# A gate branch whose product and residual sum become separate steps, with its next head begun one stage earlier and its divisions moved behind the sums

## The chip, the core and the metric

The kernel is one program for one core of a Trainium2 chip, all in fp32. The metric is the device time of one execution in microseconds, the median over the runs shown. One execution was also recorded by the hardware profiler, and all readings of single instructions come from that one.

The core has five instruction streams that each run strictly in their own order: PE (TensorE, matmuls; its weight loads are listed as PEld), DVE (VectorE), ACT (ScalarE), POOL (GpSimd) and SP (SyncE, which here only issues DMAs). An instruction that waits for another engine holds up everything behind it in its own stream.

## The reference

Two stages, each the sum of the residual and a product of two branches, over 4096 tokens (two sequences of 2048) of width 256:

```python
xn = layernorm(x)
s  = local_and_latent_attention(xn)          # first branch
g  = silu(expert_mlp(xn))                    # eight experts, one per token, layernorm at its end
x  = x + s * g
xn = layernorm(x)
s  = attention_and_mlp(xn)                   # second main branch
g  = silu(two_layers(xn))                    # second gate branch
return x + s * g

def two_layers(x):                           # DEPTH = 2, 8 heads of 64
    for l in range(2):
        h = shift_token(x)                   # second half of the channels comes from the token before
        q, k, v = split(h @ wqkv[l])
        q, k = rotary(l2norm(q) * qs, l2norm(k) * ks)
        x = x + local_attention(q, k, v) @ wo[l]          # windows of 128, looking one window back
        h = layernorm(shift_token(x)) * lg + lb
        a, b = split(h @ w1[l] + b1[l])
        x = x + (a * gelu(b)) @ w2[l] + b2[l]
    return x
```

## The kernel before

Tokens lie on the 128 partitions; a tile is 128 tokens, a group is four tiles (`GT = 4`), and there are eight groups (`NG = 8`). The whole program is three stages that follow each other.

1. The first stage, to about 966 us in the profile: for every group the attention branch (`attention(g)`), which stores its rows to the DRAM tensor `rows_s`, and between its steps the sorted tiles of the experts (`experts()`), 39 of them, which store to the DRAM tensor `ysort`.
2. The gate branch, about 966 to 2340 us: sixteen rounds (`NR = 2 * NG`), eight for layer 0 and eight for layer 1. Round r treats the four tiles of one group. Side by side in it stand `attention(r)`, the preparation (`prepare`) of the next tiles' queries and keys, the head of the next round (`gate_head(r + 1)`), and the feed-forward part of the round before (`forward(r - 1)`).
3. The main branch, to the end.

Nothing in this program is left to a scheduler on PE, DVE, ACT and POOL: each engine gets its instructions in the order in which Python emits them (the DMA issues on SP are placed by the framework). Emission order is decided by one helper, `in_turn`. It takes lanes, each a triple `(a, b, steps)`; every step has a weight, the steps of a lane are laid out over the stretch from a to b in proportion to their weights, and all steps of all lanes are then emitted in the order of these places. A step `(3, lambda: None)` emits nothing and only pushes the later ones back. In the first stage places are counted within one group (0 to 1), in the gate branch a unit is one round.

The head of a round of layer 0, `gate_head(r)` with r < 8, is where the first stage's two branches meet and the gate branch gets its input. For its four tiles it

- fetches the input rows `x` and the attention rows `sg` from `rows_s` (SP, 512 KB each),
- gathers the experts' rows `yg` from `ysort` (POOL, four indirect DMAs),
- takes Silu of `yg` in one ACT instruction over all four tiles (L370, with a table load before it),
- per tile multiplies `sg` by `yg` on POOL (L363), adds that to `x` on DVE (L364) and takes the moments (L79 and L80): these are one step, `residual(t)`,
- stores the sum to `rows_r`, forms the reciprocal deviations on POOL (`ln_rsqrt`, L84 and L85) and normalizes on DVE (L88),
- shifts half of the channels by one token with four DMAs to `xs_a` (`shift`), and transposes both halves on PE into `hT` (L384).

The tiles `sg` and `yg` have a single buffer each. For rounds of layer 1 the head is only the shift and the transposes.

In `attention(r)` a block i is half a tile. Its steps are: transposes of the softmax weights (`turn_weights(i)`, L151, copied out as `pt` by ACT and DVE in turn, L69 and L71); then `small(i)`, which is the scores of the next block (L453, softened by DVE at L107, then exponentials on ACT, L473) and the weighted sums of this one (`sum_block(i)`, L483) into two PSUM banks `acc`, of which there are exactly the two that one tile needs. The divisions of a finished tile n (`divide(n)`, DVE: L628, L629, L632) read these banks and are emitted after `turn_weights` of the next tile's first block. So the sums of a new tile may not start before the divisions of the tile before it have read the banks. `turn_out(n)` (L642) and `project_tile(n)` (L658, L667) follow.

In `prepare(m)` the engines alternate on one tile: PE projects (L530, L546), POOL makes the rotated cross terms (`cross`, L563) and a power for the lengths (`lengths`: DVE L572 and L573, then POOL L574), and DVE does the long elementwise steps (`straight` L579, `join` L587, `scale` L590). `forward` is L742, L754, L755 and L764, with L761 and L771 for its sums.

Where the lanes lay before: the head of round 0 is spread over the last group of the first stage (fetch at 0.02, gathers at 0.10, the rest from 0.30 to 0.65); every later head r + 1 lies in round r from its start to 0.45 of it. The experts take a share of each group, 0.35 of the first, all of the next six and 0.1 of the last.

Of the kernel before, what the change touches and what calls it, by code (L numbers as in the profile page):

```python
# [9 lines left out]
ALU = mybir.AluOpType  # L10
# [6 lines left out]
GT = 4  # L17
GW = GT * P
NG = NT // GT
# [11 lines left out]
def kernel(ctx: ExitStack, tc: tile.TileContext, io: dict, col: dict):  # L31
    nc = tc.nc
# [3 lines left out]
    def sb(pool, shape, tag, bufs=None):  # L36
        kw = {} if bufs is None else {"bufs": bufs}
        return pool.tile(list(shape), F32, name=tag, tag=tag, **kw)
# [4 lines left out]
    def bank(tag):  # L43
        return ps.tile([P, 512], F32, name=tag, tag="acc" if tag == "acc" else "b", bufs=2 if tag == "acc" else 6)
# [272 lines left out]
    def group(r):  # L317
        return slice((r % NG) * GT, (r % NG) * GT + GT)
# [20 lines left out]
    def gate_head(r):  # L339

        x = G[:, group(r), :]
        lane = []
        if r < NG:
            d = {}

            def fetch():

                d["mv"] = sb(ph, [P, GT, 2], "h_mv", 2)
                d["rs"] = sb(ph, [P, GT], "h_rs", 2)
                nc.sync.dma_start(x, xin[:, group(r), :])  # L350
                d["sg"] = sb(ph, [P, GT, D], "sg", 1)
                nc.sync.dma_start(d["sg"], rows_s[:, group(r), :])
                d["yg"] = sb(ph, [P, GT, D], "yg", 1)

            def gather(t):
                n = r * GT + t
                nc.gpsimd.indirect_dma_start(
                    d["yg"][:, t, :], None, ysort, bass.IndirectOffsetOnAxis(ap=ati[:, n : n + 1], axis=0)
                )

            def residual(t):

                nc.gpsimd.tensor_tensor(d["sg"][:, t, :], d["sg"][:, t, :], d["yg"][:, t, :], ALU.mult)  # L363
                nc.vector.tensor_tensor(x[:, t, :], x[:, t, :], d["sg"][:, t, :], ALU.add)  # L364
                ln_moments(ph, d["mv"], t, [x[:, t, :]])

            lane.append((0.1, fetch))
            lane += [(0.3, lambda t=t: gather(t)) for t in range(GT)]
            lane.append((3, lambda: None))
            lane.append((1, lambda: nc.scalar.activation(d["yg"], d["yg"], AF.Silu)))  # L370
            lane += [(1, lambda t=t: residual(t)) for t in range(GT)]
            lane.append((0.1, lambda: nc.sync.dma_start(rows_r[:, group(r), :], x)))
            lane.append((1, lambda: ln_rsqrt(d["rs"], d["mv"], 1e-5)))
            lane.append((2, lambda: None))
            for t in range(GT):
                lane.append((1, lambda t=t: normalize(x[:, t, :], x[:, t, :], d["mv"], d["rs"], t)))
        lane.append((0.1, lambda: shift(ph, "xs_a", r, x)))

        def turn(c):
            if r not in heads:  # L380
                heads[r] = sb(ph, [P, 2, GW], "hT", 2)
            tp = bank("tp")
            for t in range(GT):
                nc.tensor.transpose(  # L384
                    tp[:, t * P : (t + 1) * P], shifted["xs_a", r][:, t, :] if c else x[:, t, 0:P], ident
                )
            copy(c, heads[r][:, c, :], tp)

        return lane + [(1, lambda: turn(0)), (2, lambda: None), (1, lambda: turn(1))]
# [16 lines left out]

    pools = {}

    def gate_branch():
        NR, NM = 2 * NG, 2 * NT  # L410
        wo, w1, w2 = {}, {}, {}

# [199 lines left out]
        def turn_weights(i):  # L612
            turns[i] = turned(pools["tasks"], scores.pop(i))

        def sum_block(i):
            n, blk = i // 2, i % 2
            if not blk:
                accs[n] = [
                    bank("acc")[:, 0 : 4 * (DH + 1)].rearrange("p (b u d) -> p b u d", b=2, u=2) for _ in range(2)
                ]  # L620
            keys = [(m, b) for m in (n - 1, n) for b in range(2)][blk : blk + 3][3 - min(3, i % (2 * TPB) + 1) :]
            collect64(turns.pop(i), accs[n], blk, [tiles[m]["v"][:, b, :, :] for m, b in keys])

        def divide(n):
            acc = accs.pop(n)
            rz = sb(pools["tasks"], [P, 2, 2, 2], "rz")
            for w in range(2):
                nc.vector.tensor_copy(rz[:, w, :, :], acc[w][:, :, :, DH])  # L628
            nc.vector.reciprocal(rz, rz)  # L629
            o = outs[n] = sb(pools["tasks"], [P, 2, 2, 2, DH], "o")  # L630
            for w in range(2):
                nc.vector.tensor_tensor(  # L632
                    o[:, :, :, w, :], acc[w][:, :, :, 0:DH], bc(rz[:, w, :, :], 3, [P, 2, 2, DH]), ALU.mult
                )
# [41 lines left out]
        def attention(r):  # L676
            lane = []
            for i in range(2 * GT * r, 2 * GT * (r + 1)):

                n, odd = i // 2 - 1, i % 2  # L680

                def turn(i=i, n=n, odd=odd):
                    turn_weights(i)
                    if n >= 0 and not odd:
                        divide(n)

                def small(i=i):

                    if i + 1 < 2 * NM:
                        score(i + 1)  # L690
                    sum_block(i)

                lane += [(1, turn), (1, lambda: None), (1.5, small)]
                if odd:
                    lane.append((1, lambda n=n: project_tile(n) if n >= 0 else None))
                else:
                    lane += [(0.5, lambda: None), (0.5, lambda n=n: turn_out(n) if n >= 0 else None)]
            return lane
# [95 lines left out]
        lanes = []  # L794
        for r in range(NR):
            lanes.append((r, r + 1, attention(r)))
            ahead = [prepare(m) for m in range(GT * r + 2, min(GT * r + GT + 2, NM))]
            if r == NG - 1:

                ahead.insert(2, [(0, lambda: load_wqkv(1)), (4, lambda: rotation_rows(rw[1], row1)), (4, lambda: None)])  # L800
            if r == NR - 1:
                ahead.append([(0, load_c_qkv)])
                ahead.append([(1, lambda j=j: turn_tile(NM - 1, j)) for j in range(2)])
            lanes.append((r, r + (1 if r < NR - 1 else 0.5), sum(ahead, [])))
            if r < NR - 1:
                lanes.append((r, r + 0.45, gate_head(r + 1)))
            if r < NR - 2:
                lanes.append((r + 1.25, r + 2.65, forward(r)) if r < NR - 3 else (r + 1.25, r + 2.35, forward(r)))
        return [prepare(m) for m in range(2)], begin, lanes, forward(NR - 2), [step for _, step in finish(NM - 1)], forward(NR - 1)
# [6 lines left out]
    with ExitStack() as l0_ctx:  # L816
# [598 lines left out]
        scale_latent(0)  # L1415
        turn_latent(0)
        flow = experts()
        shares = [0.35, 1, 1, 1, 1, 1, 1, 0.1]
        weight = sum(w for w, _ in flow) / sum(shares)
        def experts_done():  # L1420
            right_ctx.close()
# [1 line left out]
            pools["tiles"] = tiles_ctx.enter_context(tc.tile_pool(name="tiles", bufs=2, side="right"))  # L1423

        tiles_ctx = ExitStack()
        first_tiles, begin_d, lanes_d, last_but_one, (divide_d, turn_d, project_d), last_d = gate_branch()
        due = 0
        for g in range(NG):
            lanes = [(0, 1, attention(g))]
            if g < NG - 1:  # L1430
                lanes.append((0.05, 0.75, head(g + 1)))
            if g == 0:
                lanes += [(0.09 * k, 0.09 * k + 0.2, prep(4 + k)) for k in range(4)]
                lanes += [(0.48, 0.6, route()), (0.6, 0.62, [(1, open_experts), (1, lambda: expert_load(0))])]
            share, due = [], due + weight * shares[g]
            while flow and (due > 0 or g == NG - 1):
                due -= flow[0][0]
                share.append(flow.pop(0))
            if g == NG - 1:
                share.append((0.1, experts_done))  # L1440
            if share:
                lanes.append((0 if g else 1 - shares[g], shares[g] if g == NG - 1 else 1, share))
            if g == NG - 2:
                lanes.append((0.5, 1, [(1, lambda: load_wqkv(0)), (1, load_rotation)]))
            if g == NG - 1:
                first, second = first_tiles
                (_, fetch), *rest = gate_head(0)
                lanes += [(0.02, 0.04, [(1, fetch), (1, lambda: rotation_rows(rw0, row0))])]
                at = shares[g]
                lanes += [(at, at + 0.05, rest[:GT]), (at + 0.2, at + 0.55, rest[GT + 1 :])]  # L1450
                lanes += [(0.66, 0.96, first), (0.85, 1.2, second)]
                lanes.append((1, 1.2, [(1, lambda i=i: ends[NT - 1][i]()) for i in range(6)]))
            in_turn(*lanes)
# [303 lines left out]
    with ExitStack() as end_ctx:  # L1757
# [12 lines left out]
        lanes = list(lanes_d)  # L1770
# [154 lines left out]
```

## Time and profile before

| what | value |
|---|---|
| median of three runs | 3017.39 us (3013.52 to 3017.89) |
| the profiled execution, whole | 3016.3 us |
| its span, first to last instruction | 3014.5 us |
| PE busy | 2750.4 us, 91% of the span |
| DVE busy | 1897.8 us, 63% |
| ACT busy | 1676.0 us, 56% |
| POOL busy | 1071.7 us, 36% |
| mean granted PE clock | 0.951 of full speed |

The profiled execution is 1.1 us under the median, and 1.8 us of it lie outside the span. Busy shares are averages over three stages with different limits. The windows view splits the span; in its rows "PEclk" is the share of full speed that PE was granted. In a timeline, the bracket at the end of a row gives the idle time of the engine before that instruction and what ended it. In the view of waits a row says who waited for whom, for how long in total, how often, and the longest.

### The profile page before, as it was taken

To read this page: it belongs to the slowest core of one execution; us is meant where nothing else is said; L and a number is where in the kernel's file an instruction comes from. 1 tells how busy PE (TensorE), PEld (TensorE's weight loads), DVE (VectorE), ACT (ScalarE), POOL (GpSimd) and SP (SyncE) were. 2 spreads that over 40 slices of the span, in tenths; PEclk is the share of its full clock that TensorE was granted. 3 is DMA by queue.
4 is the path that set the end of the run, shared out by engine and by line. 5 is a ranking of instruction groups with operands and counts; after the bars stand their busy time and mean duration, and the time that the engine had idled before them with its cause. 6 is when DMAs were issued, how large, how long until landed. Compare 5 with 4: busy or idle time off the path is not lost. (4 is left out here: it accounts for less than half of the span.)

```text
span 3014.5 us, 72442 instructions
## 1 busy us (share of the span) xinstructions
PE 2750.4 (91%) x28226; PEld 1981.8 (66%) x28226; DVE 1897.8 (63%) x6725; ACT 1676.0 (56%) x4587; POOL 1071.7 (36%) x1236
## 2 busy tenths in 40 slices
PE   6689999999977789999999999999998899999997
PEld 4578878788764556656666666666666566666666
DVE  5746666565656777777776666667666556555542
ACT  2347777786764444444444445554544567677672
POOL 1113333333334554545453443434433112222212
PEclk7779999999988899999999999999999999999998
DMA  4032222222202100110000000000000010000000
GB/s 147 24 108 91 79 98 85 79 98 84 78 28 79 38 28 24 29 29 16 26 26 29 15 27 16 5 8 9 5 5 20 18 41 23 22 28 23 15 16 22
DMA packets 84229, 123.59 MB, mean 41 GB/s; under 512 B 7728, under 2 KB 74448, under 8 KB 78896
## 3 DMA queue, kind: packets, MB, share of 16 engines
q1 hardware_dynamic: 80480, 109.64, 11.3%
q0 software_dynamic: 3408, 9.31, 1.1%
q8 instruction: 225, 3.69, 0.5%
q14 instruction: 116, 0.95, 0.1%
HBM read 88.65 MB, written 21.89 MB: 37 GB/s over the span
## 5 line engine op out<-in xcount | busy, mean ns | idle before, releaser
L473 ACT ACTIVATE pr<-pr,mn 128x192 f32<-128x192 f32 (+2 forms) x512 | 188.5, 439 | 276.4 <-DVE mn L107 276.1
L574 POOL TENSOR_TENSOR inv<-inv,nhalf 128x16 f32<-128x16 f32 x64 | 186.6, 2916 | 414.3 <-DVE inv L573 414.2
L107 DVE CUSTOM_DVE_ANT_0 pr<-s,cst 128x128 f32<-128x128 f32 (+2 forms) x1024 | 261.6, 315 | 95.2 <-PE s L1572 73.6
L742 PE MATMUL s<-h2T,d_w 128*128 128x512 f32 x704 | 310.8, 593 | 0.0
L69 ACT COPY pt<-tp 128x384 f32<-128x384 f32 (+3 forms) x320 | 156.8, 495 | 251.8 <-PE tp L151 216.3
L151 PE MATMUL tp<-cst,pr 128*128 128x128 f32 x1488 | 218.6, 284 | 52.3 <-ACT pr L473 48.9
L136 ACT ACTIVATE pr<-pr,mn 128x192 f32<-128x192 f32 (+2 forms) x512 | 222.9, 436 | 73.1 <-DVE mn L107 72.7
L1592 ACT ACTIVATE pr<-pr,mn 128x128 f32<-128x128 f32 x512 | 198.1, 388 | 107.8 <-DVE mn L107 107.5
L563 POOL TENSOR_TENSOR scr<-scr,tab 128x512 f32<-128x512 f32 x128 | 176.8, 1381 | 214.6 <-DVE scr L71 214.4
L530 PE MATMUL s<-d_wqkv,hT 128*128 128x512 f32 x512 | 246.3, 624 | 0.0
L71 DVE COPY pt<-tp 128x384 f32<-128x384 f32 (+3 forms) x320 | 181.2, 566 | 96.4 <-PE tp L151 66.4
L151 PEld LDWEIGHTS tp<-cst,pr 128*128 128x128 f32 x1488 | 179.6, 146 | 93.8 <-ACT pr L473 56.2
L742 PEld LDWEIGHTS s<-h2T,d_w 128*128 128x128 f32 x704 | 131.1, 190 | 148.6 <-issue 145.9
L755 DVE SCALAR_TENSOR_TENSOR u<-s,cols,ge 128x512 f32<-128x512 f32 x96 | 71.3, 747 | 200.5 <-PE s L742 122.2
L764 PE MATMUL s<-d_w,u 128*128 128x256 f32 x768 | 178.4, 382 | 0.0
L530 PEld LDWEIGHTS s<-d_wqkv,hT 128*128 128x128 f32 x512 | 98.4, 203 | 98.2 <-issue 97.8
L764 PEld LDWEIGHTS s<-d_w,u 128*128 128x128 f32 x768 | 142.6, 190 | 23.7 <-issue 4.6
L165 PE MATMUL acc<-pt,v 64*32 64x128 f32 x4992 | 122.6, 287 | 38.3 <-DVE pt L71 18.9
L1097 PE MATMUL s<-Wo,it 128*128 128x128 f32 x1248 | 157.5, 280 | 0.0
L1724 POOL TENSOR_TENSOR x<-x,stream 128x256 f32<-128x256 f32 x32 | 23.3, 727 | 374.9 <-DVE x L1723 374.9
L1097 PEld LDWEIGHTS s<-Wo,it 128*128 128x128 f32 x1248 | 148.0, 194 | 8.1 <-issue 7.4
L107 DVE CUSTOM_DVE_ANT_0 pr<-s,cst_a 128x192 f32<-128x192 f32 (+2 forms) x512 | 144.0, 346 | 11.6 <-PE s L114 8.7
(294 smaller groups left out, 6476.3 us busy)
## 6 DMA issues: line engine op xcount, KB each, us to landing
w<-in_W1b_dram SPq DMA_DIRECT2D x39, 1028.0 KB
ysort<-ys SPq DMA_DIRECT2D x39, 128.0 KB
xn<-in_L_attn_x_dram SPq DMA_DIRECT2D x8, 512.0 KB
rows_n<-xn SPq DMA_DIRECT2D x8, 512.0 KB
rows_s<-s SPq DMA_DIRECT2D x32, 128.0 KB
stream<-in_L_attn_x_dram SPq DMA_DIRECT2D x8, 512.0 KB
sg<-rows_s SPq DMA_DIRECT2D x8, 512.0 KB
rows_r<-stream SPq DMA_DIRECT2D x8, 512.0 KB
```

Source lines behind the costliest of these rows:

```text
L71: nc.vector.tensor_copy(out, in_)
L107: nc.vector.tensor_tensor_reduce(pr, sc, mask, 1.0, CAP, ALU.add, ALU.min, mn)
L136: nc.scalar.activation(w, w, AF.Exp, bias=mn[:, v : v + 1], scale=-1.0, accum_out=zs[:, v, blk, s : s + 1])
L151: nc.tensor.transpose(tp[:, k * P : (k + 1) * P], pr[:, k, :, :].rearrange("p v j -> p (v j)"), ident)
L473: nc.scalar.activation(p, p, AF.Exp, bias=mn[:, w : w + 1], scale=-1.0)
L530: nc.tensor.matmul(mm, lhsT=heads[r][:, k, t * P : (t + 1) * P], rhs=wqkv_d[l][:, k, j * INNER : (j + 1) * INNER], start=(k == 0), stop=(k ...
L563: nc.gpsimd.tensor_tensor(d["r2"][:, :, :, 32 * hf : 32 * hf + 32], d["qk"][:, :, :, 32 - 32 * hf : 64 - 32 * hf], bc(d["tab"][:, 2:4, hf, ...
L574: nc.gpsimd.tensor_tensor(inv.rearrange("p a h -> p (a h)"), inv.rearrange("p a h -> p (a h)"), nhalf, ALU.pow)
L742: nc.tensor.matmul(mm, lhsT=w1[l][:, k, c, :], rhs=d["h2T"][:, k, 0:w], start=(k == 0), stop=(k == 1))
L764: nc.tensor.matmul(mm[:, 0:D], lhsT=d["u"][:, c, i * P : (i + 1) * P], rhs=w2[l][:, c, :], start=(c == 0), stop=(c == HC - 1),)
L1097: nc.tensor.matmul(mm, lhsT=d["it"][:, ic, :], rhs=late["Wo"][:, ic, h], start=(ic == 0), stop=(ic == FF // P - 1))
L1592: nc.scalar.activation(w, w, AF.Exp, bias=mn[:, v : v + 1], scale=-1.0, accum_out=zs[:, v, blk, st : st + 1])
```

## The change

The four edits are all edits of emission order; no engine gets an instruction more or fewer, apart from where an ACT table load falls.

1. In `gate_head`, the POOL product becomes a step of its own, `product(t)`, with pauses before and after, so that all four products are emitted some way ahead of the first sum. Pauses elsewhere in the lane are longer too.
2. The lane of a head is stretched: heads 2 to 7 now begin 0.2 of a round ahead of the round in whose first half they end. The head of round 0 is spread over 0.03 to 0.62 of the first stage's last group in one lane. The head of round 1 is built before the gate branch; its first twelve steps (`AHEAD = 2 * GT + 4`: fetch, gathers, pause, Silu, pause, products) go into 0.64 to 1 of that last group, and only the rest, from the pause before the sums, into the first 0.35 of round 0.
3. `divide(n)` moves from behind `turn_weights` of the next tile's first block to right behind `sum_block` of the tile's own second block.
4. The experts' share of the last group goes from 0.1 to 0.03.

```diff
+            def product(t):
+                nc.gpsimd.tensor_tensor(d["sg"][:, t, :], d["sg"][:, t, :], d["yg"][:, t, :], ALU.mult)
+
             def residual(t):
 
-                nc.gpsimd.tensor_tensor(d["sg"][:, t, :], d["sg"][:, t, :], d["yg"][:, t, :], ALU.mult)
                 nc.vector.tensor_tensor(x[:, t, :], x[:, t, :], d["sg"][:, t, :], ALU.add)
                 ln_moments(ph, d["mv"], t, [x[:, t, :]])
 
             lane.append((0.1, fetch))
             lane += [(0.3, lambda t=t: gather(t)) for t in range(GT)]
-            lane.append((3, lambda: None))
+            lane.append((4, lambda: None))
             lane.append((1, lambda: nc.scalar.activation(d["yg"], d["yg"], AF.Silu)))
+            lane.append((2, lambda: None))
+            lane += [(0.5, lambda t=t: product(t)) for t in range(GT)]
+            lane.append((2, lambda: None))
             lane += [(1, lambda t=t: residual(t)) for t in range(GT)]
             lane.append((0.1, lambda: nc.sync.dma_start(rows_r[:, group(r), :], x)))
             lane.append((1, lambda: ln_rsqrt(d["rs"], d["mv"], 1e-5)))
-            lane.append((2, lambda: None))
+            lane.append((3, lambda: None))
...
-    def gate_branch():
+    def gate_branch(next_head):
...
-                def turn(i=i, n=n, odd=odd):
-                    turn_weights(i)
-                    if n >= 0 and not odd:
-                        divide(n)
-
-                def small(i=i):
+                def small(i=i, odd=odd):
 
                     if i + 1 < 2 * NM:
                         score(i + 1)
                     sum_block(i)
-
-                lane += [(1, turn), (1, lambda: None), (1.5, small)]
+                    if odd and i + 1 < 2 * NM:
+                        divide(i // 2)
+
+                lane += [(1, lambda i=i: turn_weights(i)), (1, lambda: None), (1.5, small)]
...
             if r < NR - 1:
-                lanes.append((r, r + 0.45, gate_head(r + 1)))
+                head = next_head if not r else gate_head(r + 1)
+                lanes.append((r - 0.2 if r and r + 1 < NG else r, r + (0.45 if r else 0.35), head))
...
-        shares = [0.35, 1, 1, 1, 1, 1, 1, 0.1]
+        shares = [0.35, 1, 1, 1, 1, 1, 1, 0.03]
...
-        first_tiles, begin_d, lanes_d, last_but_one, (divide_d, turn_d, project_d), last_d = gate_branch()
+
+        AHEAD = 2 * GT + 4
+        next_head = gate_head(1)
+        first_tiles, begin_d, lanes_d, last_but_one, (divide_d, turn_d, project_d), last_d = gate_branch(next_head[AHEAD:])
...
                 at = shares[g]
-                lanes += [(at, at + 0.05, rest[:GT]), (at + 0.2, at + 0.55, rest[GT + 1 :])]
+                lanes += [(at, 0.62, rest), (0.64, 1, next_head[:AHEAD])]
```

## Prediction

> **What bounds the kernel now.** I read the page first, then the windows view cut at the rounds, then who PE waits for in the gate branch, then one stall on three engines.
>
> ```profile
> PE   6689999999977789999999999999998899999997
> PEclk7779999999988899999999999999999999999998
> ```
>
> PE is the engine that is nearly always busy, with one hole in the middle, where the first stage hands over to the gate branch, and the granted clock falls with it. PE alone cannot say which rounds lose, so the windows, one per round:
>
> ```profile
> core 0: us, PE busy (x) PEld busy (x) DVE busy (x) ACT busy (x) POOL busy (x), PEclk, DMA share, GB/s
> 966.00:1016.00 50.00, 33.04 (x338) 20.60 (x335) 30.37 (x83) 18.48 (x39) 25.28 (x23) 0.75 0.37 118
> 1016.00:1088.00 72.00, 58.23 (x745) 40.24 (x744) 57.28 (x154) 30.68 (x64) 39.42 (x35) 0.93 0.11 31
> 1088.00:1179.00 91.00, 83.63 (x830) 55.09 (x829) 67.26 (x178) 42.62 (x76) 45.78 (x40) 0.96 0.09 24
> 1545.00:1630.00 85.00, 83.66 (x844) 56.32 (x842) 59.20 (x164) 40.40 (x74) 35.41 (x32) 1.00 0.08 26
> 1808.00:1893.00 85.00, 84.52 (x847) 57.07 (x846) 58.23 (x162) 40.54 (x74) 36.42 (x32) 1.00 0.06 17
> ```
>
> 1545 to 1630 is the first full round without a residual sum, 1808 to 1893 one of layer 1: both take 85 us, PE all but full at full clock. 1088 to 1179 is one of five alike that hold a head of layer 0: 91 us, PE idle for 7. Those five are the room, with the two stretches ahead of them. The waits of PE between 966 and 2340 us name it:
>
> ```profile
> PE tp L151 <- ACT pr L473: 48.9, 10, 10.2
> PE acc L483 <- DVE o L632: 13.7, 19, 1.5
> ```
>
> The first row is mostly the heads: 10.18 us at 995.7 (head 1), 8.38 at 1068.5 (head 2), then 5.10, 5.10, 5.59, 5.10, 5.10 (heads 3 to 7). The second is the sums waiting for the divisions to free `acc`. One stall of the first kind, POOL, then DVE, then PE:
>
> ```profile
> 1139.82 0.73 POOL L363 TENSOR_TENSOR sg<-sg,yg 128x256 f32<-128x256 f32 x1 [9.11 <-ACT yg L370]
> ...
> 1145.91 2.94 POOL L574 TENSOR_TENSOR inv<-inv,nhalf 128x16 f32<-128x16 f32 x1 [4.13 <-DVE inv L573]
> 1148.83 0.71 POOL L363 TENSOR_TENSOR sg<-sg,yg 128x256 f32<-128x256 f32 x1
> ```
> ```profile
> 1140.58 1.47 DVE L364 TENSOR_TENSOR stream<-stream,sg 128x256 f32<-128x256 f32 x1 [3.49 <-POOL sg L363]
> ...
> 1145.65 0.17 DVE L573 TENSOR_SCALAR inv<-inv 128x16 f32<-128x16 f32 x1
> 1149.58 0.98 DVE L364 TENSOR_TENSOR stream<-stream,sg 128x256 f32<-128x256 f32 x1 [3.75 <-POOL v L541]
> ...
> 1153.23 0.39 DVE L364 TENSOR_TENSOR stream<-stream,sg 128x256 f32<-128x256 f32 x1
> ```
> ```profile
> 1155.44 1.59 PE L151 MATMUL tp<-cst,pr 128*128 128x128 f32 x6 [5.10 <-ACT pr L473]
> ```
>
> The two queues hold each other up. DVE stands at the first sum until ACT's Silu and POOL's product are through. POOL's second product stands behind a power (L574), which waits for DVE's L573, which is queued behind the first sum; then the power takes 2.94 us, and DVE stands 3.75 us at the second sum. Behind the sums on DVE are the softmax maxima (L107), and behind those ACT's exponentials and PE's transposes.
>
> **The change part by part**, against the profiled execution (3016.3 us; the median is 1.1 higher).
>
> *Products apart, heads 3 to 7.* In the changed program's order on POOL all four products stand ahead of the next tile's copy, cross term and power, one tile after the gathers, and ACT's Silu between them; the first sum stands behind the maxima of another block. The circle is cut. The five rounds from 1088 to 1545 take 457 us; five of 85 would be 425, so 32 are to be had: 26.0 of waits and 6 of clock (0.96 against 1.00). Next late is DVE, which keeps the sums: an add of 0.39 us plus 0.43 and 0.18 of moments, 1.0 from start to start at 1153.23, so 4.0 per head. In the layer-1 round DVE idles 3.08 and 1.61 us in that place, waiting for `ge`, which takes them in. But L364 has a median of 0.98 and a longest of 1.48 beside POOL; four times 1.09 of stretch is 4.4 us in front of the maxima, against some 3 us by which the exponentials lead PE's L151 there. I leave 1 us per head: -27 (from -14, half stays, to -32).
>
> The Trainium skill ("SBUF — State Buffer", "Who interferes with whom") speaks against it: a DVE instruction with two SBUF inputs and a GpSimd one that reads SBUF exclude each other, and the loser is fully blocked until the other ends. The sums no longer meet 0.7 us products but could meet L574: 28 sums of heads 1 to 7 times 2.94 would be 82 us, more than the whole gain. The row decides against that size: at 1040.51 the straight step L579 (both inputs in SBUF) took 1.22 us inside a power running from 1038.67 to 1041.58, and 1.22 again at 1868.73 inside one from 1867.60; what stretches it is POOL's wide products, to 1.75 at 940.76. So I price a meeting at 1.09 us at most: 28 times that is 31 us of DVE, and the kernel before already pays most of it.
>
> *Head 2.* 72 us from 1016 to 1088, PE waits 8.4 and 1.7. No feed-forward fills these rounds, so DVE (57.3 us busy) is next: with 2 to 3 us of waits that it can't avoid the stretch is 60 to 62. -10 (-5 to -12).
>
> *Head 1.* Waits 10.18, 1.90 and 1.67 of PE from 982 to 996 at a clock of 0.75. Its four gathers (964.9 to 970.8 on POOL), the Silu with two table loads (2 x 1.28 + 1.06 us on ACT) and the products leave this stretch; the sums come free of waits but still 4 us long. -12 (-6 to -16).
>
> *Head 0.* DVE waits 5.3, 1.5 and 1.5 us for products in the tail of the first stage, and PE stands 5.7, 1.2 and 5.0 from 896 to 906. Its products now precede by half a tile. But its Silu now lies ahead of eight exponentials where ACT has 3.4 us idle (before 872.92) and needs 3.6, after gathers that end later: 2 us back. -5 (0 to -8).
>
> *Divisions.* 1.24 us of DVE each (1853.69 to 1854.93) move in front of L579. They wait for PE's sums, which follow the scores at once (1898.74 to 1899.62) while the maxima run to 1900.1: no wait is added. What is behind them, `scale` L590, ends 3 to 4 us before PE's L507 takes it (1853.3 and 1857.5; 1875.2 and 1878.3), and L587 often waits for POOL anyway (1.85 at 1871.81). PE's 13.7 + 0.7 us of waits for `o` and `rz` go; a third lies in the DVE-bound stretch of head 2 and buys nothing. -7 (+4 to -10).
>
> *What is put into the tail.* Head 1's four gathers (1.25 us each) and products (4 x 0.72) go to POOL where it idles 8.16 us ahead of L1356 at 933.39 and 8.23 ahead of 957.03; if that cover failed, 8 us. ACT's 3.6 us meet an idle 7.5 at 951.85. The SP order of fetches, stores and shifts stays as it was: `sg` is refetched only when the last sum frees it (905.5, 994.3, 1067.2), its consumer is most of a round away. Of the experts' weight (7.3 each, 39 of them) 3.1 move from the last group to full ones, 0.42 of an expert; with 149.7 + 157.5 + 16.4 us of PE for 39 that is 3.5 us, mostly taken from the same engine's time in the tail. +4 (0 to +9).
>
> Sum: -27 - 10 - 12 - 5 - 7 + 4 = -57: 3016.3 becomes 2959.3, a median of 2960. The ends are -78 and -12.
>
> **Rivals.**
> *The sums become the wait.* DVE, moved out of POOL's way, is itself late with 4 to 8 us of sums ahead of the maxima, and half of heads 1 to 7 stays (25 of 49), with little at head 0. For: DVE is 67 of 91 us busy there, and 57 of 72 in the thin rounds. Against: layer 1's idle DVE in that place. About -30: 2987.
>
> *It does not come apart.* The first product waits for Silu, and Silu for the gathers; if these set the time, the wait only moves. For: the wait of POOL for `yg` is 9.11 in the row above. Against: POOL reached that product early and just stood there; Silu's own wait for the gathers is 1.0 us in all, and gathers now start most of a round before the sums. About 0: 3017.
>
> *Slower: the divisions lie bare.* 63 of them stand 1.24 us in front of the rotation steps; if `scale` had no lead over PE, that is 78 us, 3038 with the rest gained. It decides from 57 / 63 = 0.9 us each. Against: the leads of 3 to 4 us. For: the thin rounds, where DVE has little to spare.
>
> *More than the sum*: all waits gone and the clock at 1.00 through the hand-over, below 2942.
>
> **How the numbers follow.** Forecast 0.70 (2942 to 2975), sums late 0.18, more than the sum 0.05, no effect 0.02, bare divisions 0.05. The range from 2940 to 2994 takes in the forecast's spread and most of the first rival, and leaves out the rest. Faster by more than 0.2% (6 us, about what this kernel's measurement can tell): 0.93; within 0.02; slower 0.05.
>
> **What would show it.** Right: no wait of DVE L364 for POOL L363 of more than 1 us in rounds 1 to 6; PE's L151 waiting for ACT under 15 us in the gate branch instead of 48.9; L483 waiting for `o` under 3; rounds of 85 to 87 us at a clock of 0.99 from 1.5 rounds on; the same 85 in layer 1. Wrong: those rounds still at 90, with L107 late behind L364 (sums late); L507 waiting for `scr` L590 in many tiles (bare divisions); a first stage longer by more than 5 us (the tail).

## The result, and the profile after

The changed kernel takes 2980.68 us (median, 2977.69 to 2984.06), the kernel before, beside it, 3015.45: a ratio of 0.9886, with a 95% interval from 0.9868 to 0.9903. It is 35 us faster; the forecast was 57. The profiled execution took 2981.85 us, its span is 2980.1.

The page first: the hole in PE's row is narrower and shallower, and the granted clock recovers sooner.

```profile
PE   6789999999987899999999999999998999999997
PEclk7789999999988999999999999999999999999999
```

The windows, one per round (after the time: busy time and count of each engine, then the clock granted to PE):

```profile
core 0: us, PE busy (x) PEld busy (x) DVE busy (x) ACT busy (x) POOL busy (x), PEclk, DMA share, GB/s
955.00:1005.00 50.00, 37.04 (x346) 22.09 (x346) 34.97 (x91) 15.55 (x37) 24.00 (x20) 0.83 0.33 107
1005.00:1071.00 66.00, 57.44 (x742) 41.11 (x742) 55.44 (x153) 30.55 (x63) 40.35 (x35) 0.95 0.12 34
1159.00:1251.00 92.00, 87.50 (x847) 58.11 (x846) 66.35 (x179) 42.94 (x76) 47.98 (x42) 0.98 0.09 24
1523.00:1608.00 85.00, 84.19 (x867) 56.97 (x869) 61.22 (x165) 40.52 (x74) 36.94 (x31) 1.00 0.09 26
1778.00:1862.00 84.00, 83.89 (x846) 56.78 (x845) 59.72 (x161) 40.53 (x74) 37.97 (x32) 1.00 0.06 17
```

The surprise is the third of these rows, one of the five rounds that hold heads 3 to 7: 92 us, of which PE shows 87.5 busy. It was to become 85 to 87. Yet the waits that the change was to remove are gone, or nearly. The waits of PE from 955 us to the end of the gate branch:

```profile
PE acc L488 <- DVE pt L71: 11.4, 14, 3.2
PE tp L151 <- ACT pr L478: 10.0, 7, 2.7
PE tp L389 <- DVE stream L88: 9.7, 6, 3.2
...
PE acc L488 <- issue: 6.1, 14, 0.5
PE s L458 <- DVE x L672: 4.8, 5, 2.6
```

L151's wait for ACT fell from 48.9 us to 10.0, and the wait of PE's weighted sums (L488) for `o` is gone; their wait for `pt` grew, from 3.4 us to 11.4. On DVE the residual sums of the head show it (groups of instructions; after the bar busy time, mean ns of one, and the idle time ahead). Before:

```profile
L364 DVE TENSOR_TENSOR stream<-stream,sg 128x256 f32<-128x256 f32 x32 | 32.5, 1015 | 59.4 <-POOL sg L363 48.1 <-POOL v L541 11.3
```

After:

```profile
L366 DVE TENSOR_TENSOR stream<-stream,sg 128x256 f32<-128x256 f32 x32 | 13.1, 410 | 0.0
```

59.4 us of waiting became none, and a sum takes 410 ns instead of 1015. So the circle is cut as forecast, and in the rounds it was aimed at that bought almost nothing. Measured from the gate branch's first `x1` tile of a round (L667 before, L672 after) to that of the next, in the two profiled executions:

```
stretch                                      before    after   difference   forecast
start to a step late in the first stage       954.4    949.0      -5.4         -1
from there to round 0's first tile, head 1     61.5     55.6      -5.9        -12
round 0, head 2                                72.3     67.0      -5.3        -10
rounds 1 to 5, heads 3 to 7                   456.6    451.8      -4.8        -27
rounds 6 to 14, no head                       780.3    767.1     -13.1         -7
round 15 and the main branch                  689.5    689.6       0.1          0
```

The rows sum to 34.4 us. The first two part where DVE starts the last addition but two to the first stage's rows (L1376 before, L1379 after); those rows are all stored some 12 us later in both kernels. The row to explain is the fourth: five waits of 5 us left these rounds, and they are hardly shorter.

### The profile page after: what moved, and what is told of

It reads as the page before. It is cut to its first block, busy times and chain, and to the rows that moved or that the text cites. A ratio compares the mean times of both kernels' runs of the same rounds, so it can differ in the third digit from the quotient of the medians.

```text
span 2980.1 us, 72390 instructions
## 1 busy us (share of the span) xinstructions
PE 2745.5 (92%) x28226; PEld 1979.7 (66%) x28226; DVE 1900.0 (64%) x6725; ACT 1676.8 (56%) x4587; POOL 1090.0 (37%) x1236
## 4 chain that ended last, share of the span: by engine, by line
PE 64%; DVE 15%; ACT 11%; issue 5%; POOL 4%; DMA 1%; SPq 0%; POOLq 0%; DVEq 0%; ACTq 0%
PE s L744 10%; PE s L535 5%; PE s L766 4%; PE s L1100 4%; PE tp L151 4%; PE s L1083 3%; PE s L1725 3%; ACT pr L136 3%; PE s L663 3%; ACT pr L1598 3%; PE s L551 2%; PE s L1712 2%; DVE pr L107 2%; PE s L458 2%; PE acc L488 2%
## 5 line engine op out<-in xcount | busy, mean ns | idle before, releaser
L744 PE MATMUL s<-h2T,d_w 128*128 128x512 f32 x704 | 317.3, 603 | 0.4 <-ACT pr L478 0.4
L535 PE MATMUL s<-d_wqkv,hT 128*128 128x512 f32 x512 | 237.3, 605 | 0.0
L568 POOL TENSOR_TENSOR scr<-scr,tab 128x512 f32<-128x512 f32 x128 | 168.2, 1314 | 184.6 <-DVE scr L71 184.5
L744 PEld LDWEIGHTS s<-h2T,d_w 128*128 128x128 f32 x704 | 133.4, 193 | 153.3 <-issue 151.8
L151 PE MATMUL tp<-cst,pr 128*128 128x128 f32 x1488 | 214.8, 280 | 15.8 <-ACT pr L478 10.0
L151 PEld LDWEIGHTS tp<-cst,pr 128*128 128x128 f32 x1488 | 178.2, 144 | 55.7 <-issue 22.7
```

Source lines behind the costliest of these rows:

```text
L151: nc.tensor.transpose(tp[:, k * P : (k + 1) * P], pr[:, k, :, :].rearrange("p v j -> p (v j)"), ident)
L535: nc.tensor.matmul(mm, lhsT=heads[r][:, k, t * P : (t + 1) * P], rhs=wqkv_d[l][:, k, j * INNER : (j + 1) * INNER], start=(k == 0), stop=(k ...
L568: nc.gpsimd.tensor_tensor(d["r2"][:, :, :, 32 * hf : 32 * hf + 32], d["qk"][:, :, :, 32 - 32 * hf : 64 - 32 * hf], bc(d["tab"][:, 2:4, hf, ...
L744: nc.tensor.matmul(mm, lhsT=w1[l][:, k, c, :], rhs=d["h2T"][:, k, 0:w], start=(k == 0), stop=(k == 1))
```

## The experiments

Times are medians, ratios are to the kernel before on the same chip. One profiled execution differs from another by a few us ahead of round 0 even where two kernels issue the same instructions there (its first tile lies at 1004.6 us in the changed kernel, at 1000.5, 1006.8, 1002.5 and 1012.1 in gathers_late, root_late, both_late and start_back below), so the rounds are compared by their own lengths.

### Gathers: two tests of one cause

In one round of the changed kernel, PE and POOL (start, duration, group; in brackets the idle time ahead and what ended it):

```profile
1178.05 0.88 PE L458 MATMUL s<-kT,qT 64*64 64x192 f32 x16
1178.75 1.51 PE L488 MATMUL acc<-v,pt 64*64 64x65 f32 x39
1180.67 0.34 PE L488 MATMUL acc<-v,pt 64*64 64x65 f32 x3 [0.41 <-issue]
1181.40 0.30 PE L488 MATMUL acc<-v,pt 64*64 64x65 f32 x2 [0.39 <-issue]
1182.16 0.35 PE L488 MATMUL acc<-v,pt 64*64 64x65 f32 x4 [0.46 <-issue]
```
```profile
1176.47 1.89 POOL L357 DMA_INDIRECT yg<-ysort,ati  x1 [0.17 <-issue]
1178.66 1.01 POOL L357 DMA_INDIRECT yg<-ysort,ati  x1 [0.30 <-issue]
1179.97 0.95 POOL L357 DMA_INDIRECT yg<-ysort,ati  x1 [0.30 <-issue]
1181.22 0.95 POOL L357 DMA_INDIRECT yg<-ysort,ati  x1 [0.30 <-issue]
```

A block's 48 sums (L488), issued within 0.66 us in the median of all blocks, took 3.5 us here, in trickles, with no semaphore behind the gaps ("issue"). The lane's earlier start had put the four gathers on top of this burst in every one of heads 2 to 7 (2.2 to 3.6 us each time); in the kernel before they lay among the feed-forward's wide matmuls for heads 3 to 7. Behind the burst PE ran at half clock for 3.4 us: four matmuls (L744) took 1.7 us more between them, 0.42 us each for three. That is a second part of the cost, but not of the gathers alone: in root_late below they lie at the same place, and this stretch of half clock is gone.

**gathers_late**: only POOL's order changes.

```diff
+            if r > 1:
+                lane.append((3, lambda: None))
             lane += [(0.3, lambda t=t: gather(t)) for t in range(GT)]
-            lane.append((4, lambda: None))
+            lane.append((4 - 3 * (r > 1), lambda: None))
```

> The changed kernel with nothing moved but the four row gathers of heads 2 to 7, on POOL only: from just before a block's sums on PE (L488) to 7 us later, into the wide matmuls of the feed-forward; no other queue changes its order. Theory A (the gathers' transfers starve PE of its many short matmuls): six bursts of 48 sums go from 2.2 to 3.6 us back to 0.66, 15 us in all, plus some of the half-clock matmuls behind them: 2961 to 2967, a ratio to the kernel before of 0.982 to 0.984, and the 'issue' waits of L488 (6.1 us) go. Theory B (those bursts are slow for a reason of their own, such as where their code lies): 2981 as before the edit, 0.9886. Theory C (the gathers starve whatever lies beside them): the wait moves to L744, and the time stays within 4 us of 2981.

2970.1 us, ratio 0.9853 (0.9838 to 0.9868; the change's interval begins where this one ends). In its trace the same burst:

```profile
1173.52 0.53 PE L490 MATMUL acc<-v,pt 64*64 64x65 f32 x24
1174.23 0.58 PE L490 MATMUL acc<-v,pt 64*64 64x65 f32 x24 [0.18 <-DVE pt L71]
```

The trickle is gone, though the first gather still runs there; "issue" waits of L488 fall from 6.1 to 0.4 us, and nothing took their place at L744 (theory C falls). Rounds 1 to 5 take 432.5 us instead of 451.8. The median fell by 10.6 us, less than the 14 to 20 expected and less than these rounds did; the profiled execution, the fastest of the four (2960.68), fell by 21.

**before_gathers_early**: the kernel before, with the gathers of heads 2 to 7 alone where the changed kernel has them; again only POOL's order changes.

```diff
-            lane.append((3, lambda: None))
+            lane.append((12 if 1 < r else 3, lambda: None))
...
-                lanes.append((r, r + 0.45, gate_head(r + 1)))
+                lanes.append((r - 0.2 if r and r + 1 < NG else r, r + 0.45, gate_head(r + 1)))
```

> The kernel before with nothing moved but the gathers of heads 2 to 7, on POOL only, a fifth of a round earlier, to where the changed kernel has them (just before a block's sums, L483). Theory A: five bursts of heads 3 to 7 lengthen from 0.66 to some 3.5 us, head 2's was disturbed already: 3027 to 3035, a ratio of 1.004 to 1.0065. Theory B or C: within 4 us of the kernel before, 0.999 to 1.0015. It also shows the price that the change paid for the lanes' earlier start.

3027.01 us, ratio 1.0031 (1.0017 to 1.0044): slower, by 11 us, the lower edge of what theory A expected. The trickle appears where there was none:

```profile
1204.05 1.47 PE L483 MATMUL acc<-v,pt 64*64 64x65 f32 x42 [0.63 <-DVE rz L629]
1205.91 0.31 PE L483 MATMUL acc<-v,pt 64*64 64x65 f32 x2 [0.39 <-issue]
1206.64 0.51 PE L483 MATMUL acc<-v,pt 64*64 64x65 f32 x4 [0.42 <-issue]
```

The bursts of heads 3 to 7 last 2.0 to 2.8 us. Taken away and put in, the gathers' place is worth 11 us either way: theory A holds, B falls.

**plain_rows**: what in a gather does it? The same queue, place and bytes, without indices.

```diff
-                nc.gpsimd.indirect_dma_start(
-                    d["yg"][:, t, :], None, ysort, bass.IndirectOffsetOnAxis(ap=ati[:, n : n + 1], axis=0)
-                )
+                if r < 2:
...
+                else:
+                    nc.gpsimd.dma_start(d["yg"][:, t, :], ysort[n * P : (n + 1) * P, :])
```

> The changed kernel with the gathers of heads 2 to 7 made plain transfers of as many rows, on the same queue at the same place; it reads the experts' rows in their stored order, so the gate's input is another one. Theory A1 (the bytes that move, or the transfers' descriptors, starve PE beside them, whatever their kind): the six bursts of L488 stay at 2.2 to 3.6 us and the time at 2978 to 2983. Theory A2 (it is the indirect kind, whose addresses are worked out as it runs): the bursts fall to 0.66 and the time to 2966 to 2971, as when the gathers were moved.

2963.36 us, ratio 0.9832 (0.982 to 0.9845), rounds 1 to 5 at 432.0: A2, and 3 us better than it expected. The burst, with the transfers ahead of it:

```profile
1173.85 1.20 PE L491 MATMUL acc<-v,pt 64*64 64x65 f32 x48
```
```profile
1171.35 2.23 POOL L362 DMA_DIRECT2D yg<-ysort  x4
```

Issued within 0.99 us (heads 4 to 7; 1.34 and 1.46 for heads 2 and 3), while the DMA engines moved 216 GB/s, against 111 beside the gathers' burst above. So it is not the rate of the bytes that holds PE up. What differs is the indirect kind, and with it the issuing: the four plain transfers were issued by 1173.58, before the burst began, where POOL was still issuing three of the gathers during theirs. Which of the two does it, this kernel doesn't tell. A late fetch of instructions is not seen: beside the bursts of heads 5 and 7 in the changed kernel the two DMA queues that the profile calls "instruction" move no packet, and the packets of the larger one beside heads 4 and 6 take 0.88 and 0.99 us, where its median is 1.02.

### The head's inverse root

The second cost of these rounds is a queue. The changed kernel, POOL, DVE and PE:

```profile
1225.46 1.22 POOL L84 TENSOR_SCALAR h_rs<-h_mv 128x4 f32<-128x4 f32 x1
1226.76 1.01 POOL L85 TENSOR_TENSOR h_rs<-h_rs,nhalf 128x4 f32<-128x4 f32 x1
1227.74 1.27 POOL L568 TENSOR_TENSOR scr<-scr,tab 128x512 f32<-128x512 f32 x1
```
```profile
1229.04 1.73 DVE L592 TENSOR_TENSOR scr<-scr 128x1024 f32<-128x1024 f32 x1 [2.42 <-POOL scr L568]
1230.70 0.41 DVE L672 TENSOR_TENSOR x<-s,stream 128x256 f32<-128x256 f32 x1
```
```profile
1231.16 0.88 PE L458 MATMUL s<-kT,qT 64*64 64x192 f32 x16 [0.57 <-DVE x L672]
...
1233.29 0.58 PE L488 MATMUL acc<-v,pt 64*64 64x65 f32 x24 [0.90 <-DVE pt L71]
...
1237.08 0.33 PE L389 MATMUL tp<-cst,stream 128*128 128x128 f32 x1 [1.42 <-DVE stream L88]
```

The sums now finish early, so the head's inverse root (L84, L85) comes to stand in front of the tile's cross term L568; DVE stands 2.42 us at L592, and PE waits 2.9 us in three places.

**root_late**: one swap in POOL's queue.

```diff
+            if r > 1:
+                lane.append((0.5, lambda: None))
             lane.append((1, lambda: ln_rsqrt(d["rs"], d["mv"], 1e-5)))
-            lane.append((3, lambda: None))
+            lane.append((3 - 0.5 * (r > 1), lambda: None))
```

> The changed kernel with one swap in POOL's queue for heads 2 to 7: the head's inverse root (L84, L85, 2.2 us) behind the second cross term L568 that DVE's L592 waits for, not ahead of it. Theory D (the root in front of the cross term is what holds DVE, and through it PE at L458, L488 and L389): the 2.4 us wait of DVE goes and PE gains 2 to 3 us in five or six rounds: 2965 to 2971, a ratio of 0.983 to 0.985. Rival E (DVE itself is full there with the head's sums and normalizations, so the same PE waits end on the next DVE instruction): 2977 to 2981. Rival F (the normalizations, now later, hold the turn of the head L389 longer): 2981 to 2990.

2971.18 us, ratio 0.9852 (0.9837 to 0.9867): 9.5 us less, just above what D expected. Rounds 1 to 5 take 441.0, 10.8 less. But only one of the three places is cured: L458's wait for L672 (4.8 us in all up to round 5) is gone from the list, L488's for `pt` falls from 9.4 to 7.9, and a part of F came with it: the waits at the head's turn rose from 9.7 to 12.6 us. The queue's waits are the smaller part of the gain; the larger is clock, as the five rounds show below.

**both_late**: both moves in one kernel.

> The changed kernel with both moves, the gathers of heads 2 to 7 into the wide matmuls and the inverse root behind the cross term. If A and D hold and add up: 2945 to 2957, a ratio of 0.977 to 0.981, and the five rounds of heads 3 to 7 at 86 to 87 us instead of 88 to 93. If only one of them holds: 2961 to 2971. If neither: 2981.

2956.84 us, ratio 0.9812 (0.9797 to 0.9826). They add up: 10.6 and 9.5 alone, 23.8 together, and the five rounds at 427.8, that is 83.7 to 86.6 each, all at full clock; one of them:

```profile
1154.00:1240.00 86.00, 83.33 (x844) 56.35 (x843) 65.88 (x175) 42.97 (x76) 47.89 (x42) 1.00 0.09 26
```

Against the kernel before that is 29 us less in these five rounds: the forecast's 27 was there to be had.

**turn_late**: what is left in them is PE's wait at the turn of the head, which stands ahead of work that PE could do.

```diff
-        return lane + [(1, lambda: turn(0)), (2, lambda: None), (1, lambda: turn(1))]
+        hold = 0 if not 0 < r < NG else 1.5 if r == 1 else 1
+        return lane + [(hold, lambda: None), (1, lambda: turn(0)), (2 - hold, lambda: None), (1, lambda: turn(1))]
```

> The kernel with both moves (gathers and inverse root late) and one more: the turn of a head's first half on PE (four transposes, L389 of the changed kernel), for heads 1 to 7, a step later, behind the feed-forward's narrow matmuls and the next turn of weights; the copy of it moves one place on DVE. Theory G (the turn stands ahead of work that PE could do while DVE still normalizes: waits of 3.2 us at head 1 and 1.4 to 1.5 us at the other six): they go, 2945 to 2950, ratio 0.977 to 0.9785. Rival H (DVE is full in that stretch and the next thing it owes PE, the weights' copies or the later copy of the turned head, is late instead): 2955 to 2960, as with the two moves alone.

2952.43 us, ratio 0.9805 (0.9792 to 0.9818), between what G (2945 to 2950) and H (2955 to 2960) expected. The waits at the turn fall from 12.8 to 2.5 us and the five rounds to 419.1 in the profiled execution, 81.6 to 84.8 each, what a layer-1 round takes. The interval still meets that of both_late: its gain over that kernel is seen in the trace but not settled by the times. It is the fastest of all, 2% ahead of the kernel before.

### The five rounds, taken apart

Rounds 1 to 5 in the profiled executions, in the order before, changed, gathers_late, root_late, both_late, turn_late:

```profile
1088.16:1544.74 456.58, 425.55 (x4151) 283.24 (x4150) 334.61 (x880) 212.84 (x380) 231.41 (x205) 0.96 0.09 26
1071.53:1523.33 451.80, 428.09 (x4152) 285.93 (x4151) 328.23 (x880) 213.06 (x380) 236.17 (x205) 0.98 0.09 26
1069.47:1501.97 432.50, 415.62 (x4151) 280.18 (x4150) 328.10 (x880) 212.93 (x379) 236.89 (x205) 1.00 0.10 27
1071.75:1512.71 440.96, 421.45 (x4152) 282.16 (x4151) 328.67 (x880) 213.20 (x380) 235.27 (x205) 1.00 0.10 26
1069.82:1497.58 427.76, 413.82 (x4152) 278.57 (x4151) 328.55 (x881) 213.22 (x380) 235.95 (x205) 1.00 0.10 27
1065.20:1484.30 419.10, 412.20 (x4150) 278.42 (x4149) 324.98 (x881) 212.69 (x380) 240.59 (x205) 1.00 0.10 28
```

PE idle is the length less PE's busy time. The clock lost is half of the time that PE was busy while its granted clock was 0.50.

```
us                      before   changed   gathers_late   root_late   both_late   turn_late
PE idle                   31.0      23.7           16.9        19.5        13.9         6.9
lost to half clock        11.7       8.0            1.7         1.7           0           0
the rest of PE busy      413.9     420.1          413.9       419.7       413.8       412.2
```

With the gathers beside the short matmuls PE is busy some 6 us longer for the same work, which is the trickle. Moving them takes these 6 us, 7 of idle time and 6 of lost clock. Moving the inverse root takes 4 us of idle time and 6 of lost clock. Why the clock stays up in root_late, with the bursts as long as before, no run tells.

### One part of the change undone

**joined**: each product in front of its own sum again, all places in the lane kept.

```diff
-            def product(t):
-                nc.gpsimd.tensor_tensor(d["sg"][:, t, :], d["sg"][:, t, :], d["yg"][:, t, :], ALU.mult)
-
             def residual(t):
 
+                nc.gpsimd.tensor_tensor(d["sg"][:, t, :], d["sg"][:, t, :], d["yg"][:, t, :], ALU.mult)
...
-            lane += [(0.5, lambda t=t: product(t)) for t in range(GT)]
+            lane += [(0.5, lambda: None) for t in range(GT)]
```

> The changed kernel with each product put back in front of its own sum in the lane, all pauses kept, so that lanes, gathers, Silu and sums stay where they are; only POOL's order changes. If cutting the circle between POOL's products and DVE's sums is what took PE's waits at L151 away, they return (48.9 us in the kernel before, 10.0 after): 3000 to 3015, ratio 0.995 to 1.000. If the earlier lane start alone (Silu long done when the sums come) did it, the four products cost DVE little: 2981 to 2990.

2998.7 us, ratio 0.9951 (0.9938 to 0.9964), between the two expectations. The circle is back, but at one sum per head of heads 2 to 7, since the Silu is long done: there a product stands behind the power again, and DVE 3.70 us at its sum.

```profile
1222.61 2.90 POOL L577 TENSOR_TENSOR inv<-inv,nhalf 128x16 f32<-128x16 f32 x1 [9.63 <-DVE inv L576]
1225.47 0.72 POOL L363 TENSOR_TENSOR sg<-sg,yg 128x256 f32<-128x256 f32 x1
```
```profile
1226.23 0.43 DVE L364 TENSOR_TENSOR stream<-stream,sg 128x256 f32<-128x256 f32 x1 [3.70 <-POOL sg L363]
```

PE's waits at L151, up to round 5, are 20.8 us against 8.3: 1.7 to 2.0 in each of the five rounds, not 5, and 4.7 at head 2. Rounds 1 to 5 take 458.7 us, so joining the products gives back all that the change won there. The trace names 8 us of the 18 by which the median rises (its profiled execution was the fastest of the five, 2989.96), 6.9 of them in these rounds; the rest is not accounted for.

**start_back**: products and sums apart, but the lanes at their round again.

```diff
-                lanes.append((r - 0.2 if r and r + 1 < NG else r, r + (0.45 if r else 0.35), head))
+                lanes.append((r, r + (0.45 if r else 0.35), head))
```

> The changed kernel with the lanes of heads 2 to 7 started at their round again, not a fifth of a round earlier, products and sums still apart; gathers, Silu, products and sums all come later and closer together, and the gathers lie in the wide matmuls again. If cutting the circle is enough by itself, the time falls as with the gathers late, to 2966 to 2972, ratio 0.983 to 0.985. If the earlier start is needed for the Silu and the products to be done before the sums, PE's waits at L151 return in part, 2980 to 2990, ratio 0.988 to 0.991.

2991.03 us, ratio 0.9916 (0.9902 to 0.9929): 10 us above the change's median, though the two intervals just touch, and though its gathers lie in the wide matmuls again. Two products wait for Silu and two stand behind the power, the sums come late, and PE pays at L488 and L458 (15.7 and 5.7 us up to round 5) more than at L151. So the early start is needed: with the gathers in the wide matmuls either way, rounds 1 to 5 take 449.7 us here and 432.5 in gathers_late. Net of what it paid for the gathers it bought nothing in these rounds (451.8 in the changed kernel), and 3 us at head 2 (67.0 against 69.9). Of the 12.7 us between the two profiled executions 7.5 lie ahead of round 0's first tile, where both issue the same instructions; so the traces do not show the 10 us of the medians to be the early start's.

**divide_back**: only DVE's order changes.

```diff
-                    if odd and i + 1 < 2 * NM:
-                        divide(i // 2)
...
+                def turn(i=i, n=n, odd=odd):
+                    turn_weights(i)
+                    if n >= 0 and not odd:
+                        divide(n)
```

> The changed kernel with its divisions back in front of the next tile's turn of weights; only DVE's order changes. By the forecast's term for the divisions the time rises by 7 us, to 2988; by the round-by-round account of the two traces (the rounds from 7 on hold no head and are 12 us shorter) by 12 or more, to 2992 to 2998, ratio 0.992 to 0.994. Rival (bare divisions: they cost what they gain): 2981, or less.

2993.95 us, ratio 0.9933 (0.9917 to 0.9948): 13 us, as the account of the rounds had it. Rounds 6 to 14 take 780.6 us, again what they took before the change. Up to round 5 the weighted sums wait 14.2 us for `o` and `rz` and not for `pt`; in the changed kernel they wait 9.4 us for `pt` instead.

**head1_back** and **share_back**: head 1's first half back in round 0; the last share 0.1.

```diff
-                lanes += [(at, 0.62, rest), (0.64, 1, next_head[:AHEAD])]
+                lanes += [(at, 0.62, rest)]
...
-        first_tiles, begin_d, lanes_d, last_but_one, (divide_d, turn_d, project_d), last_d = gate_branch(next_head[AHEAD:])
+        first_tiles, begin_d, lanes_d, last_but_one, (divide_d, turn_d, project_d), last_d = gate_branch(next_head)
...
-                lanes.append((r - 0.2 if r and r + 1 < NG else r, r + (0.45 if r else 0.35), head))
+                lanes.append((r - 0.2 if r and r + 1 < NG else r, r + 0.45, head))
```
```diff
-        shares = [0.35, 1, 1, 1, 1, 1, 1, 0.03]
+        shares = [0.35, 1, 1, 1, 1, 1, 1, 0.1]
```

> The changed kernel with head 1 wholly in its first full round again, as in the kernel before, its gathers, Silu and products with it; head 0 and the other heads stay. By the forecast's term (12 us for head 1's stretch, its cost in the tail covered) the time is 2991 to 2995, ratio 0.992 to 0.993; by the account of the traces (that stretch 5.9 us shorter, the tail 8.7 us shorter in spite of what was put into it) 2985 to 2989. Rival (the tail pays what the first round gains): 2979 to 2983.

> The changed kernel with the experts' shares as before (0.1 of a group in the last one, not 0.03); the lane of head 0 follows the share, as it does in the kernel. The forecast's term (+4 for the full groups, covered by the tail) makes this 2977; the account by tiles (groups 1 to 6 are 6.5 us longer after the change, the tail 8.7 shorter) leaves open how much of the tail's gain is the share's: 2972 to 2976 if none of it, 2981 to 2984 if the share's own time in the tail is what the groups pay.

2981.49 us, ratio 0.9898 (0.9883 to 0.9913), and 2982.74, ratio 0.9899 (0.9885 to 0.9913): both meet the change's own interval. Neither part can be told from nothing. With head 1 back in its round the 10.18 us wait does not return; PE waits 1.52, 1.48 and 2.99 us there, where the change has 2.10, 0.83 and 3.21.

## Why the forecast was right in sign and 22 us off

*Products apart, heads 3 to 7, forecast -27, measured -4.8.* The step that failed is "Next late is DVE, which keeps the sums", with its reserve of 1 us per head: the list of what comes late next held only the sums. The sums cost nothing. What came next was POOL's queue on both sides of them. The gathers, moved earlier with the lane, were counted as four instructions on POOL with slack behind them, and not by what PE does while they run: 11 us, by two kernels. The inverse root came up early with the sums and took its place in front of the cross term: 9.5 us, by one kernel, in the trace more by the clock than by the waits. With both out of the way the five rounds are 29 us shorter than before the change. The forecast's "6 of clock" was also misread. It is what was left of 32 us after the waits, but a clock of 0.96 over 457 us is some 18 us of clock time, and 11.7 of matmul time was lost to it; five rounds of 85 us were not the floor either, as turn_late's 419.1 show.

*Head 2, forecast -10, measured -5.3.* The gathers account for 1.6 us of burst. No kernel came near the 60 to 62 us: in the changed one and the ten made from it the stretch stayed between 65 and 70, with waits that wander from L151 to L488 and back, and DVE 55 us busy in the changed one. That DVE bounds it, as the first rival has it, fits this but was not tested.

*Head 1, forecast -12, measured -5.9, and for another reason.* Taking its gathers, Silu and products out of the stretch is worth nothing that the times can tell (head1_back). With the products joined again, and its first half still in the tail, no sum of head 1 waits either (joined). So the one part or the other, or the longer pauses that both kernels keep, is enough to end the long wait; the forecast counted the stretch's removed work as well, and of that nothing shows. The new wait of 3.21 us at the head's turn was not foreseen.

*Head 0, the tail and the experts' share, forecast -1 together, measured -5.4.* Too mixed, and too near to what executions differ by ahead of round 0, to name a part; share_back moves nothing that can be measured.

*Divisions, forecast -7, measured -13.* The waits for `o` went, and `scale` was late only where it had been before (6.6 us once at the end, against 5.4). But waits for `pt` came in part for those for `o`, so that PE's idle time in rounds 6 to 14 falls by only 3.4 us. What was left out is the clock: PE lost 5.6 us there to half clock before, and 1.5 after. The other 5.6 us lie within PE's busy time and are not taken apart. Most of it all is round 7, in which PE stood 1.5 and 1.2 us for `o`. It ran at a clock of 0.96 before, and at 1.00 after.

```profile
1630.00:1722.00 92.00, 86.35 (x795) 58.14 (x794) 57.85 (x162) 39.58 (x75) 36.38 (x31) 0.96 0.05 13
```
```profile
1608.00:1694.00 86.00, 81.64 (x780) 54.82 (x773) 58.40 (x163) 39.44 (x74) 37.05 (x31) 1.00 0.05 14
```

PE's busy time falls by 4.7 us, with 795 and 780 matmuls in the two windows. This round takes 91.5 to 91.8 us in the three kernels with the divisions in their old place, and 85.3 to 88.1 in all the others. From before to after it is 6.2 us shorter: 1.3 of idle time, since a wait of 1.4 us for `pt` stands where one for `o` did, and 3.4 of clock, from 6.8 us at half clock to none. The new place alone does not keep the clock up: gathers_late, with the same waits there, has 6.8 us at half clock in this round and takes 88.1.

*The rule weighed*, mutual exclusion of DVE's sums and POOL's reads: it cost next to nothing here. In six meetings of a sum with a power the sum takes 0.42 us, like the median of all; the power, which began second each time, takes 3.00 to 3.01 instead of 2.93. The other order is in start_back, in five heads:

```profile
1229.10 2.94 POOL L579 TENSOR_TENSOR inv<-inv,nhalf 128x16 f32<-128x16 f32 x1 [5.57 <-DVE inv L578]
```
```profile
1231.21 0.41 DVE L366 TENSOR_TENSOR stream<-stream,sg 128x256 f32<-128x256 f32 x1
```

The sum begins 2.1 us into the power and ends 0.4 us ahead of it, so it was not blocked until the other's end; what a sum meets in a power's first 2 us, no run shows. What does stretch it is POOL's products: 0.94 us for the next sum there, which begins inside a pair of them. The price of 1.09 per meeting with a power, which the forecast held in reserve, was not paid.

*The rivals.* The number nearest was that of "the sums become the wait" (2987), but not its mechanism: the sums wait for nothing and delay nothing. Bare divisions did not come.

## What to carry to other kernels

A step moved earlier takes its transfers and its queue neighbours with it: look at what runs on the other engines at the new place, not only at whether the moved instruction's own engine is free there. When a wait goes and the time stays, list the stretch's start-to-start times of the bound engine and look for gaps that no semaphore ends, then for the first instruction that the freed engine now waits for; here each was cured by one move in POOL's queue. Beside PE's waits, count its time at half clock: in these five rounds it cost 11.7 us before the change, and the change left 8.0 of them.

## What the runs showed that was not expected

An indirect gather slows a run of short matmuls beside it: 48 of them, issued within 0.66 us in the median, took 2.0 to 3.6 us beside four gathers of 128 KB each, and 0.99 to 1.46 us beside plain transfers of the same bytes from the same queue. Beside the wide matmuls of the feed-forward (10 or 11 of them in the time of four gathers in the kernel before, 0.43 us from start to start) no gap appears. The Trainium skill ("SBUF — State Buffer", "Who interferes with whom") has it that a DMA never contends with a compute engine and that PE never waits for anyone; for SBUF's ports that may stand, but the trace shows PE held up beside a gather by something that no semaphore records. What it is, the gathers' transfers or POOL's issuing of them, and what of PE it holds up, no run here tells.
